# A gated layer's variance taken once per token, with tokens on partitions, and brought back by products with the identity

## The chip, the cores and the metric

The kernel runs on one core of one Trainium2 chip. The metric is the device time of one execution in microseconds (us): the median of three runs for the kernel before. A profiled execution, taken apart from these runs, gives the times of single instructions.

## The reference, cut to what matters

An image batch x of shape (4, 48, 256, 256) passes through four layers, each of the form x = x + layer(group_norm(x)). Layer 0 is a channel attention after a 3x3 depthwise convolution. Layer 1 is the gated layer that the change touches. Layers 2 and 3 are scans: down, up, right and left over the image with a five-tap convolution in each step. Of layer 1:

```python
t = x.reshape(B, H * W, dim)                   # 48 consecutive numbers of memory are one token
t = gelu(gelu(t @ W1 + b1))                    # 16 features per token
x1, x2 = t[..., :8], t[..., 8:]
n = (x2 - mean(x2)) / sqrt(var(x2) + 1e-5)     # over the 8 features of one token
sp = depthwise3x3(n) + dw_b; ch = pointwise(n) + pw_b
out = (x1 * (sp * ch)) @ W2 + b2
```

All arithmetic is in float32.

## The kernel before, in words

**Stages.** `layers01` first forms the attention's matrices of all four batches, and then, as a convolution with folded weights, layer 0's output y. The convolution is cut into 64 blocks of 16 image rows (4 batches of 16). Each block is done in two halves, each with full products (L581, tile py from x1n), smaller ones (L590, py from x2n), an add into y (L604) and its statistics (L605). The first 16 blocks run alone. The other 48 are interleaved with layer 1. `scans` does layers 2 and 3, in two chains (pairs of batches), each step six TensorE products (L1067, tile ps) and two adds on VectorE (L1071, L1075). The first chain begins under the last items of layer 1.

**The gated layer.** `gated_layer` works on 32 items of 32 image rows, 8 items a batch. With 16 strips of 8 features on the 128 partitions and 512 tokens of each strip along the free dimension, an item has tiles of 128x512. One call of `tick(c, ...)` does these steps for three items at once:

- for item c+1: `load` (the DMA to tok), `relay` (GpSimd's copy to pairs, L745), and `transposed` (six ptok tiles, 4 transposes each, L751, copied to xt by VectorE at L757 or ScalarE at L755);
- for item c: `hidden` (tile ph, L698, and Gelu on ScalarE, L768 to L779), `centered` (tile pm, L785: the mean over 8 features by a product with mean8; d on VectorE, L787; its square sq on GpSimd, L789), and `normed` (the part that changes, L791 to L807), which ends with ScalarE writing n (L801) and small DMAs of edge rows to near (L811 to L820);
- for item c-2: `shift` (GpSimd, L824), `gate` (psp and pch, L830 to L833, then sp and g), `output` (tiles pout, L868, and the adds into y, L879, in two parts), the DMA of y to x2, and `finish` (eight statistics, L900).

Four calls of `conv` in each tick put four convolution halves, that is two blocks, among these steps, as long as there are blocks left. After that a tick holds only its own steps and what a scan offers.

In `normed` before, L794 multiplies sq by mean8, a 128x128 matrix that averages each 8 neighbouring partitions and writes the average to all 8. So the variance of a token stands 8 times in pvar, and the root (L796, ScalarE), the reciprocal (L797, VectorE) and the product with d (L799, VectorE) are all on 128x512.

**Order and buffers.** The code calls the steps in the order of `tick`, and a scheduler decides each engine's final order when the kernel is built, by priorities and dependencies. Each engine then executes its own instructions in order. Wherever an instruction waits, everything behind it in that engine's queue waits too. The PSUM tiles named ph, pm, pvar, psp, pch, pout, ptok, and half of those named py, share a ring of 5 banks (pool `a_banks`, tag "bank"). sq and v have one buffer each. ScalarE loads a table of functions when it changes between Gelu and the root. In the profile such a load is named ACT_TABLE_LOAD. A float32 product is recorded as two TensorE passes.

Of the kernel before, what the change touches and what calls it, by code (L numbers as in the profile page):

```python
# [9 lines left out]
F32 = mybir.dt.float32  # L10
# [7 lines left out]
G = 16  # L18
# [9 lines left out]
F = 8  # L28
# [620 lines left out]
def gated_layer(ctx, tc, banks, p_small, x1, x2, w1, w2, dw, ends, pw, cols, b2, k, coef1, coef2):  # L649
# [6 lines left out]
    nc = tc.nc  # L656
    wp = ctx.enter_context(tc.tile_pool(name="t_w", bufs=1))
    tok = ctx.enter_context(tc.tile_pool(name="t_tok", bufs=1))
    feat = ctx.enter_context(tc.tile_pool(name="t_feat", bufs=2))
# [3 lines left out]
    CH = 2 * W  # L663
# [66 lines left out]
    h1s, h2s, ds, sqs, gs, xrs, ys, stats = {}, {}, {}, {}, {}, {}, {}, {}  # L730
# [59 lines left out]

    def normed(c):  # L791
        b, j = items[c]
        pv = banks.tile([128, CH], F32, tag="bank", name="pvar")
        nc.tensor.matmul(pv, lhsT=k["mean8", 128], rhs=sqs.pop(c), start=True, stop=True)  # L794
        v = feat.tile([128, CH], F32, tag="v", name="v", bufs=1)
        nc.scalar.activation(v, pv, AF.Sqrt, bias=eps)  # L796
        nc.vector.reciprocal(v, v)  # L797
        d = ds.pop(c)
        nc.vector.tensor_mul(d, d, v)  # L799
        n = n_sb[c % NN]  # L800
        nc.scalar.activation(  # L801
            n[:, :, 1 : W + 1].rearrange("p k (t q) -> p k q t", q=4),
            by_token(d),
            AF.Identity,
            bias=col[:, 3:4],
            scale=col[:, 2:3],
        )  # L807

        here, a, z = near[c % NN], slice(0, F), slice(F, 2 * F)
        top, last = n[0:F], n[128 - F : 128]  # L810
        nc.sync.dma_start(here[a, 1, :], last[:, 0, :])  # L811
        nc.sync.dma_start(here[z, 0, :], top[:, 1, :])
        if j == 0:
            nc.sync.dma_start(here[a, 0, :], zeros)
        else:
            nc.sync.dma_start(near[(c - 1) % NN][z, 1, :], top[:, 0, :])
        if j == NJ - 1:
            nc.sync.dma_start(here[z, 1, :], zeros)
        else:
            nc.sync.dma_start(near[(c + 1) % NN][a, 0, :], last[:, 1, :])  # L820
# [85 lines left out]
    def tick(c, conv, alone):  # L906
# [40 lines left out]
        if now:  # L947
            pieces.append(lambda: normed(c))
# [654 lines left out]
```

## Time and profile before

| | us |
|---|---|
| median of 3 runs (lowest to highest) | 8981.94 (8981.17 to 8982.99) |
| the profiled execution's own time | 8983.88 |
| its span, first to last instruction | 8982.1 |
| mean granted TensorE clock in it | 0.983 of full |
| busy in the span: PE, DVE, ACT, POOL | 8646.3, 4167.5, 3479.8, 1948.9 |
| `normed` for one item: L794's two passes, L796, L797, L799 | 1.02, 0.69, 3.34, 0.67 |

How to read it: PE is TensorE's matmuls, PEld its weight loads, DVE VectorE, ACT ScalarE, POOL GpSimd, SP the engine that issues most DMAs. L797 is line 797 of the kernel. A group is named by line, engine, operation, and output tile <- input tiles, followed by the shapes, the count, the busy time, the mean of one in ns, and the idle time of the engine just before these instructions with what ended it. A timeline line has the start in us, the length, and the same name, where x8 means eight instructions merged. In the list of waits, a line gives who waited for whom, the total in us, how often, and the longest. The slices are 40 equal parts of the span, with the busy share in tenths. Passes overlap in the records, so the spacing of two passes is less than the length of one. The gated layer's items run from about 2000 to about 3550 us. Convolution blocks are among them until about 3180 us.

### The profile page before, as it was taken

Reading aid. Unit: us, or ns where it says so; the run is one execution under the profiler, and the core shown is the slowest. Engines: PE = TensorE matmul, PEld = TensorE weight load, DVE = VectorE, ACT = ScalarE, POOL = GpSimd, SP = SyncE. Lnnn points to the kernel's source line nnn. Section 1 sums busy time; section 2 is a strip of 40 time slices with the busy share of each in tenths; the row PEclk is TensorE's granted clock in tenths of the full one; section 3 lists DMA queues with packets and bytes.
Section 4 is the critical chain, followed back from the end, with each engine's and each line's share of the span. In section 5 each row is a group of like instructions: output and inputs, shape, how many; then the busy total and the mean of one; then the engine's idle time right before and its main releaser. Section 6 shows DMA issues by size and latency. Waiting matters only on the chain. (4 is left out here: it accounts for less than half of the span.)

```text
span 8982.1 us, 162711 instructions
## 1 busy us (share of the span) xinstructions
PE 8646.3 (96%) x62920; PEld 7223.1 (80%) x62920; DVE 4167.5 (46%) x15625; ACT 3479.8 (39%) x7023; POOL 1948.9 (22%) x3100
## 2 busy tenths in 40 slices
PE   6999999999999978999999999999999999999998
PEld 4777777533333335999999999999999999999998
DVE  3231110234555555445666444445666555444653
ACT  0010101123433455766601776666663003665610
POOL 0000000001111111001454000001445664101575
PEclk9999999999999988999999999999999999999998
DMA  7654323367888876765577664556656887867789
GB/s 152 132 125 94 74 61 77 82 140 160 173 181 182 182 165 162 168 138 143 155 190 190 152 139 120 141 135 141 169 146 175 216 220 181 198 172 191 210 176 183
DMA packets 1180233, 1390.64 MB, mean 155 GB/s; under 512 B 263184, under 2 KB 1107216, under 8 KB 1118784
## 3 DMA queue, kind: packets, MB, share of 16 engines
q1 hardware_dynamic: 1179360, 1379.90, 65.7%
q8 instruction: 493, 8.08, 0.4%
q14 instruction: 284, 2.33, 0.1%
q0 software_dynamic: 96, 0.33, 0.0%
HBM read 811.21 MB, written 509.61 MB: 147 GB/s over the span
## 5 line engine op out<-in xcount | busy, mean ns | idle before, releaser
L1067 PE MATMUL ps<-carry,w 96*96 96x128 f32 x48960 | 5423.7, 273 | 59.3 <-DVE carry L1071 29.1
L1067 PEld LDWEIGHTS ps<-carry,w 96*96 96x96 f32 x48960 | 5397.6, 163 | 95.0 <-issue 44.9
L1264 POOL COPY pre<-col 96x256 f32<-96x256 f32 x1020 | 657.5, 646 | 2682.2 <-DMA col<-last 1964.1
L1153 ACT ACTIVATE dn<-carry,b 96x128 f32<-96x128 f32 (+1 forms) x2044 | 769.0, 398 | 796.8 <-DVE carry L1071 789.0
L1291 ACT ACTIVATE lines<-carry,b 96x128 f32<-96x128 f32 (+1 forms) x2044 | 819.8, 402 | 583.9 <-DVE carry L1075 574.0
L1071 DVE TENSOR_TENSOR carry<-ps,dn 96x128 f32<-96x128 f32 x2280 | 653.2, 288 | 806.1 <-PE ps L1067 781.2
L1199 ACT ACTIVATE up<-carry,b 96x128 f32<-96x128 f32 x1792 | 719.5, 402 | 459.9 <-DVE carry L1071 459.6
L1075 DVE TENSOR_TENSOR carry<-ps,lines 96x128 f32<-96x128 f32 x2040 | 576.8, 286 | 562.8 <-PE ps L1067 552.9
L1075 DVE TENSOR_TENSOR carry<-ps,pre 96x128 f32<-96x128 f32 x2040 | 586.7, 288 | 457.6 <-PE ps L1067 402.4
L1071 DVE TENSOR_TENSOR carry<-ps,up 96x128 f32<-96x128 f32 x1792 | 516.0, 288 | 598.1 <-PE ps L1067 592.8
L1339 POOL TENSOR_TENSOR stage<-stage,carry 96x256 f32<-96x256 f32 x768 | 657.4, 857 | 470.4 <-DVE seen L1044 436.7
L581 PE MATMUL py<-x1n,wy 128*96 128x512 f32 x1536 | 703.1, 607 | 30.9 <-ACT x1n L541 28.4
L295 PE MATMUL acc<-xs,xt 128*96 128x288 f32 x2048 | 667.2, 408 | 0.0
L294 PE MATMUL acc<-xt 128*96 128x288 f32 x2048 | 666.8, 409 | 0.0
L581 PEld LDWEIGHTS py<-x1n,wy 128*96 128x96 f32 x1536 | 244.2, 165 | 454.7 <-issue 437.1
L279 DVE COPY xt<-pt 128x384 f32<-128x384 f32 x256 | 136.7, 555 | 849.0 <-PE pt L276 645.8
L261 ACT ACTIVATE xn<-raw,coef 96x2048 f32<-96x2048 f32 x64 | 133.7, 2095 | 987.0 <-PE pt L276 819.6
L296 PE MATMUL acc<-xt,xs 128*96 128x192 f32 x2048 | 502.1, 327 | 0.0
L296 PEld LDWEIGHTS acc<-xt,xs 128*96 128x96 f32 x2048 | 332.4, 165 | 154.5 <-issue 1.8
L295 PEld LDWEIGHTS acc<-xs,xt 128*96 128x96 f32 x2048 | 332.2, 165 | 151.4 <-issue 2.8
L604 DVE TENSOR_TENSOR y<-py,t 96x512 f32<-96x512 f32 x256 | 171.4, 678 | 593.3 <-PE py L590 584.4
L590 PE MATMUL py<-x2n,wy 64*96 64x512 f32 x1536 | 363.0, 601 | 0.0
(186 smaller groups left out, 5542.7 us busy)
## 6 DMA issues: line engine op xcount, KB each, us to landing
stage<-x SPq DMA_DIRECT2D x64, 1536.0 KB
dn<-x SPq DMA_DIRECT2D x240, 384.0 KB
R<-lines SPq DMA_DIRECT2D x60, 1536.0 KB
lines<-R SPq DMA_DIRECT2D x60, 1536.0 KB
D<-dn SPq DMA_DIRECT2D x56, 1536.0 KB
up<-D SPq DMA_DIRECT2D x56, 1536.0 KB
U<-up SPq DMA_DIRECT2D x224, 384.0 KB
col<-U SPq DMA_DIRECT2D x56, 1536.0 KB
```

The costliest lines, as they stand in the source:

```text
L294: nc.tensor.matmul(acc[0], lhsT=xt[:, h + 2, :], rhs=xt[:, here, :], start=first, stop=last)
L295: nc.tensor.matmul(acc[1], lhsT=xt[:, h + 2, :], rhs=xs[:, here, :], start=first, stop=last)
L296: nc.tensor.matmul(acc[2], lhsT=xs[:, h + 2, :], rhs=xt[:, past, :], start=first, stop=last)
L581: nc.tensor.matmul(ps, lhsT=held["w"][0][:, dx], rhs=x1n[:, 2 * c : 2 * c + 2, dx : dx + W], start=dx == 0, stop=False)
L1067: nc.tensor.matmul(ps, lhsT=w_sb[layer][:, way, j, :], rhs=old[:, i, j : j + W // 2], start=j == 0, stop=j == 2)
L1071: nc.vector.tensor_add(new[:, i].rearrange("p (k w) -> p k w", w=KC), ps.rearrange("p (k w) -> p k w", w=KC), inp[:, i])
L1075: nc.vector.tensor_add(new[:, i], ps, inp[:, i])
L1153: nc.scalar.activation(inp[:, b], blocks(new[:, b]), AF.Identity, bias=bias[:, 0:1])
L1199: nc.scalar.activation(place[:, b], blocks(new[:, b]), AF.Identity, bias=bias[:, 1:2])
L1264: nc.gpsimd.tensor_copy(t, cols_view(block)[:, :, w % 2, :, w // 2])
L1291: nc.scalar.activation(line[:, b], new[:, b], AF.Identity, bias=bias[:, 2:3])
L1339: nc.gpsimd.tensor_add(to, to, new)
```

## The change

The variance is formed once per token, with tokens on partitions. sq is now the stationary operand, cut into four parts of 128 tokens, and the moving one is 16 columns of mean8 (each eighth column). The result, pvar, has 128 tokens on partitions and 4x16 values each, so root and reciprocal work on 128x64 instead of 128x512. GpSimd then copies each value 8 times into a new tile `wide` (128x512, one buffer), and four products with `wide` as the stationary operand and the identity as the moving one turn it back to features on partitions, in a new PSUM tile pstd of the same ring. The product with d reads pstd from PSUM where it read v from SBUF.

```diff
-        pv = banks.tile([128, CH], F32, tag="bank", name="pvar")
-        nc.tensor.matmul(pv, lhsT=k["mean8", 128], rhs=sqs.pop(c), start=True, stop=True)
-        v = feat.tile([128, CH], F32, tag="v", name="v", bufs=1)
+
+        pv = banks.tile([128, 4, G], F32, tag="bank", name="pvar")
+        sq = sqs.pop(c)
+        for q in range(4):
+            nc.tensor.matmul(
+                pv[:, q], lhsT=sq[:, 128 * q : 128 * q + 128], rhs=k["mean8", 128][:, 0:128:F], start=True, stop=True
+            )
+        v = feat.tile([128, 4, G], F32, tag="v", name="v", bufs=1)
         nc.scalar.activation(v, pv, AF.Sqrt, bias=eps)
         nc.vector.reciprocal(v, v)
+        wide = feat.tile([128, 4, G, F], F32, tag="wide", name="wide", bufs=1)
+        nc.gpsimd.tensor_copy(wide, v.unsqueeze(3).to_broadcast([128, 4, G, F]))
+        pb = banks.tile([128, 4, 128], F32, tag="bank", name="pstd")
+        for q in range(4):
+            spread = wide[:, q].rearrange("p g f -> p (g f)")
+            nc.tensor.matmul(pb[:, q], lhsT=spread, rhs=k["ident", 128], start=True, stop=True)
         d = ds.pop(c)
-        nc.vector.tensor_mul(d, d, v)
+        nc.vector.tensor_mul(d, d, pb.rearrange("p q n -> p (q n)"))
```

Lines of the changed kernel behind this place are 11 higher than before: the scans' products are L1078 there, pout L879.

## The prediction

> **What bounds the kernel now.** I read the page's busy times and slices first, then stretches of the span with the granted clock, then TensorE's waits, then the order of time through one tick of the gated layer.
>
> ```profile
> PE 8646.3 (96%) x62920; PEld 7223.1 (80%) x62920; DVE 4167.5 (46%) x15625; ACT 3479.8 (39%) x7023; POOL 1948.9 (22%) x3100
> PE   6999999999999978999999999999999999999998
> ```
>
> The group of the reciprocal in 1700 to 3000 us:
>
> ```profile
> L797 DVE RECIPROCAL v<-v 128x512 f32<-128x512 f32 x19 | 63.5, 3340 | 1.1 <-ACT v L796 1.1
> ```
>
> TensorE is busy 96% of the span and in nearly all slices: it is the bound, and a microsecond on its in-order queue is a microsecond of the span unless it replaces an idle one. The reciprocal that the change shrinks costs 3.34 us a tick, but on VectorE, which is half idle. So I ask what TensorE gains or loses.
>
> ```profile
> 2090.00:3180.00 1090.00, 1032.05 (x3795) 385.21 (x3794) 582.51 (x1006) 432.78 (x425) 163.38 (x327) 0.99 0.82 178
> 3180.00:3582.00 402.00, 318.31 (x1586) 174.37 (x1581) 230.12 (x505) 209.51 (x293) 67.03 (x73) 0.84 0.73 161
> ```
>
> Columns: stretch, length, busy of PE, PEld, DVE, ACT, POOL, granted clock, DMA share, GB/s. The first stretch holds 21 ticks (items 2 to 22, some 52 us each) in which the convolution's matmuls fill TensorE: only 58 us idle, 2.8 a tick. The second holds the last nine, with no convolution left: 84 us idle.
>
> ```profile
> PE py L581 <- ACT x1n L541: 27.9, 33, 1.1
> PE ptok L751 <- POOL pairs L745: 10.2, 12, 1.7
> ...
> PE ptok L751 <- DVE y L879: 4.6, 18, 1.0
> ...
> PE ptok L751 <- DVE y L879: 17.2, 6, 3.5
> ```
>
> These are TensorE's waits (total, times, longest), three of the first stretch and, last, one of the second. Only the waits on y have the reciprocal behind them (the y adds queue after it): 4.6 us, then 17.2 us in six waits.
>
> ```profile
> 2191.66 1.02 PE L794 MATMUL pvar<-sq,cst 128*128 128x512 f32 x2
> 2192.62 2.00 PE L868 MATMUL pout<-g,w_sb 32*96 32x512 f32 x8
> 2192.47 1.28 ACT L796 ACT_TABLE_LOAD   x1
> 2193.76 0.69 ACT L796 ACTIVATE v<-pvar,eps 128x512 f32<-128x512 f32 x1
> 2194.94 3.34 DVE L797 RECIPROCAL v<-v 128x512 f32<-128x512 f32 x1
> 2339.36 0.61 PE L718 MATMUL pstrip<-spread,cst 96*128 96x16 f32 x2 [2.31 <-DVE strip L720]
> 2339.81 1.95 PE L751 MATMUL ptok<-cst,pairs 128*128 128x128 f32 x8
> 2343.66 6.59 PE L581 MATMUL py<-x1n,wy 128*96 128x512 f32 x12
> ```
>
> In one tick, pvar is followed at once by pout: TensorE waits for nothing that root and reciprocal make. The last three lines are elsewhere: after 2.31 us without work, eight ptok passes take 1.95 us (1.09 otherwise) and twelve py passes 6.59 (5.36 otherwise). The stretch 2339.2 to 2346.0 has a granted clock of 0.51.
>
> **What the skill says.** "TensorE: Matmul & The Clock Gate", section "What's actually happening": activity is judged in windows of about 3.4 us, and the clock is halved after an idle one. The trace agrees in size (a wait of 2.31 us, then 6.8 us at half clock) but shows that less than a whole idle window is enough. The same page, "LDWEIGHTS (loading the stationary operand)": the load goes by weight columns, 128 / 1.2 = 107 ns, whatever the contraction depth. The trace: eighteen pw passes (L453, 48 moving columns, 128 weight columns) take 2.10 us, that is (2.10 - 0.27) / 17 = 0.108 us apart, with 0.27 for the last one's length. "ScalarE: Activation LUTs", "What ACT_TABLE_LOAD costs": 1283 ns and a drain of 1380 more. The trace has the 1.28 but no drain: the root starts 1.29 us after its load.
>
> **Part by part.** The order in which the changed kernel is compiled is known without a run, and decides this. In ticks 2 to 22 TensorE's queue reads ptok, pvar, pstd, pout, with nothing between pvar and pstd. pstd needs wide, wide needs v, v needs pvar: TensorE, in order, stands still for the round trip, and pout, the next py and ptok stand behind it.
>
> *Work on TensorE.* Removed: two passes of 512 columns, (5.36 - 0.61) / 11 = 0.43 us apart, 0.86. Added: pvar as four products, each two passes, with sq as weights of 128 columns: 8 x 0.11 = 0.9 although only 16 columns move; pstd 8 x 0.11 = 0.9. Net +0.93 us a tick.
>
> *The round trip.* The waits on both table load and root change place: in the compiled order the load itself waits for TensorE (before, it ran while pvar did). From pvar's end: 1.28 load; the root on 64 columns 0.31, on a line from 96x1 at 0.257 (L97) to 128x512 at 0.687; reciprocal 0.55, on a line from 96x1 at 0.156 (L98) to 128x512 at 3.339; POOL's copy: contiguous copies give 0.344 (128x192) and 0.396 us (96x256), 0.81 ns an element, so 0.60 for 512, while a strided one (L1264) takes 0.646 for 256, so 1.3: I take 0.65, near the low end, since the writes are contiguous. Four handovers of 0.03 to 0.08 make 0.2. Sum 3.0, and 0.16 that the last pass's length (0.27) exceeds its spacing (0.11): 3.15. VectorE is no later: its five operations ahead of the reciprocal end about 3.2 us after py's last pass, the root about 3.8. The compiled order has no load in three ticks (6, 14, 22), so the mean is 2.95. Bounds 2.6 to 3.6.
>
> *The clock.* In the second stretch, five waits of 2.84 to 3.5 us on y were followed by half-clock stretches of 3.4 or 6.8 us. The price read above: 0.86 + 1.23 = 2.1 us for one of 6.8 us. I take 1.9 per wait; bounds 1.0 and 2.8.
>
> *What gives way.* The idle that stood later in the tick: x1n's normalization now runs during the round trip or during ph (the compiled order moves pm behind a convolution half), so its 27.9 go; the 4.6 on y go, as the reciprocal no longer delays y; half of the 10.2 on pairs, as transfers get longer ticks. 37.6 / 21 = 1.8 us a tick; bounds 0.8 and all 2.8.
>
> *Sum, ticks 2 to 21.* 2.95 + 1.9 + 0.93 - 1.8 = 4.0 us, by 20 = 80. In tick 22 the wait lies ahead of a 21.2 us wait for y's transfers, which hides it: 0. Ticks 0 and 1 have 3.6 and 5.3 us of py between pvar and pstd, so work alone: 2.
>
> *Ticks 23 to 31.* Scan matmuls fill the gap (from 5.8 down to 1.8 us) in six of them; none or nearly none in 24, 29 and 30. Added: work 9 x 0.93 = 8.4; three waits near 3.0 with their clock, 14.6; the short cover of tick 26, 3.2; remnants 0.8. Removed: 17.2 on y and its clock, 5 x 1.9. Net 0, within 15 either way. POOL's copy joins a queue that is busy 15%: hidden, except on the round trip. PSUM's ring of five banks turns one bank further each tick: pout's last tile takes pvar's bank, free since the root, and the next ptok takes pstd's, free 0.7 us after pstd when d's product has read it, while pout alone runs 2.0 us: nothing. v's and wide's single buffers are reused a tick later: nothing; were pb's reader late by its own operations on VectorE, ptok would wait for it. SP's DMAs of the edge rows are the same ones, started at about the same point. The scans' compiled order on TensorE from row 4311 of 12412 is identical, so nothing further is due.
>
> Total +82 on the span of 8982.1: 9064. The profiled execution took 8983.9, and the median of the runs is 8981.9, 0.2 below the span, so **9063** as a median.
>
> **The rivals.** *Faster, by VectorE's relief:* in the second stretch all TensorE waits on y (24.7, 17.2 and 4.0 us) might come from a late VectorE; without the reciprocal they and their clock drops (9.5) go: -55, with +18 for work and remnants: -37. It decides if the first stretch costs less than 37 / 20 = 1.85 us a tick, that is if round trip and clock together stay below 1.85 + 1.8 - 0.93 = 2.7 us (a load hoisted ahead of pvar as before and an unbroken clock would do it). At a steady cost near 0: 8945. Against: 21.2 of the 24.7 is one wait for transfers, and the load waits on TensorE in the compiled order. *No change, transfers pace the stage:* the DMA share is 0.82, and a TensorE that waits for its transfers anyway could absorb the round trip. Then 8985. Against: transfers account for only 10.2 us of TensorE's waits in 1090. *Slower still:* a broadcast read on POOL as dear as the strided copy (3.6), 2.8 for the clock, only 0.8 given back: 6.5 x 20 + 2 + 15 = 147, so 9130. The change does do what it says: the compiled reciprocals are 128x64.
>
> **How the numbers follow.** Chances: forecast 0.74, faster 0.05, no change 0.06, slower still 0.15. About 0.2% (18 us) is what a measurement of this kernel can tell from no change. Low end: 2.6 + 1.0 + 0.93 - 2.8 = 1.7 a tick, by 20, plus 2, less 15 in the late ticks: +21, rounded out to 9000. High end into the slower case, 9125. Left out: both rivals on the low side and half of the slow one, 0.19.
>
> **What would show it.** Right: TensorE waits before pstd, named POOL wide, near 3 us in some 20 ticks; granted clock from 2090 us to item 22 near 0.95 instead of 0.99 (some 5 us at half in 57); waits on x1n nearly gone; pvar passes 0.11 apart; reciprocal near 0.55. Wrong: a wait below 2 us, a clock that stays at 0.99, or x1n's waits beside the new one.

## The result and the profile after

The changed kernel takes 9103.53 us (median of 4 runs, 9099.06 to 9109.92), the kernel before 8981.56 beside it on the same chip (4 runs, 8972.99 to 8982.99). The ratio is 1.0141, with a 95% interval of 1.0129 to 1.0154. The forecast was 9063, in a range of 9000 to 9125: the side and the range hold, but the growth was 122 us where 82 was forecast. The profiled execution took 9101.23 us, its span is 9099.4, 117 us more than before; the sums by stage below are of these profiled spans.

The page of the changed kernel, busy times and slices, first. TensorE is as full as before over the whole span, but six slices fall below nine tenths where two did; VectorE lost 84 us and the span grew all the same.

```profile
PE 8690.1 (96%) x63368; PEld 7290.3 (80%) x63368; DVE 4083.0 (45%) x15625; ACT 3459.6 (38%) x7023; POOL 1962.0 (22%) x3132
PE   6999999999888878999999999999999999999998
```

The two stretches that the forecast read, now in the changed kernel (columns as there):

```profile
2090.00:3180.00 1090.00, 969.06 (x3648) 391.22 (x3647) 474.97 (x896) 371.45 (x377) 152.00 (x307) 0.92 0.75 159
3180.00:3582.00 402.00, 330.49 (x1635) 171.97 (x1634) 196.11 (x442) 190.43 (x248) 83.26 (x102) 0.87 0.75 163
```

In 1090 us TensorE is busy 969 instead of 1032, at a granted clock of 0.92 instead of 0.99, and it gets through fewer passes. Since the changed kernel is later in its work at the same time, I count from here on by items: from the start of item 2's pvar to that of item 22's (twenty ticks, the first stretch), then to 30 us after item 31's pvar (the late ticks), then the rest.

| span of | before | after | difference |
|---|---|---|---|
| start to item 2's pvar | 2139.2 | 2133.5 | -5.7 |
| first stretch, twenty ticks | 1044.8 | 1174.9 | +130.1 |
| late ticks | 342.1 | 332.9 | -9.2 |
| rest (scans) | 5456.1 | 5458.2 | +2.1 |
| all | 8982.1 | 9099.4 | +117.3 |

So all of the growth is in the first stretch, 6.5 us a tick. The waits of TensorE there, in the changed kernel (who waited for whom, total us, times, longest):

```profile
PE ptok L751 <- POOL pairs L745: 70.9, 19, 4.2
PE pstd L808 <- POOL wide L804: 59.4, 20, 3.1
PE pstrip L718 <- DVE strip L720: 4.3, 2, 2.2
```

The second line is the forecast wait: 2.97 us, twenty times. The waits on x1n (27.9 us before), on y (4.6) and on xt ahead of pout (8.6 in 13 waits) are gone. The first line is a surprise. It was 10.2 us before, and I had let half of it vanish; it is now the largest.

One tick of the changed kernel in order of time, with the engines of the round trip and, ahead of it, what leads to the wait on pairs:

```profile
2290.92 1.12 PE L785 MATMUL pm<-h,cst 128*128 128x512 f32 x2
2292.94 0.67 DVE L787 TENSOR_TENSOR d<-h,pm 128x512 f32<-128x512 f32 x1
2293.70 1.04 POOL L789 TENSOR_TENSOR sq<-d 128x512 f32<-128x512 f32 x1 [8.09 <-DVE d L787]
2294.68 2.87 POOL L745 COPY pairs<-tok 128x1536 f32<-128x1536 f32 x2
2296.20 1.97 PE L751 MATMUL ptok<-cst,pairs 128*128 128x128 f32 x8 [4.15 <-POOL pairs L745]
...
2308.89 0.96 PE L797 MATMUL pvar<-cst,sq 128*128 128x16 f32 x8
2309.93 1.28 ACT L801 ACT_TABLE_LOAD   x1 [7.36 <-PE pvar L797]
2311.22 0.31 ACT L801 ACTIVATE v<-pvar,eps 128x64 f32<-128x64 f32 x1
2311.57 0.55 DVE L802 RECIPROCAL v<-v 128x64 f32<-128x64 f32 x1 [0.32 <-ACT v L801]
2312.26 0.61 POOL L804 COPY wide<-v 128x512 f32<-128x512 f32 x1 [1.79 <-DVE v L802]
2312.92 1.77 PE L808 MATMUL pstd<-cst,wide 128*128 128x128 f32 x8 [3.07 <-POOL wide L804]
2314.62 2.04 PE L879 MATMUL pout<-g,w_sb 32*96 32x512 f32 x8
```

The lower half is the forecast chain, link by link: load 1.28, root 0.31, reciprocal 0.55, copy 0.61, and 3.07 us in which TensorE does nothing. pstd then takes 1.77 us for what takes 1.15 in pm_early_warm, a run below in which TensorE doesn't stop ahead of it. The upper half was not forecast. pm ends at 2292.04; VectorE has work of the convolution (L605, L604) to do first, so d is begun at 2292.94; GpSimd's queue holds sq and then pairs. GpSimd has been idle for 8.09 us when d ends and sq starts, with pairs behind it, and TensorE waits 4.15 us for the first half of pairs. In the kernel before, pairs did not start behind sq but when its own transfer had landed:

```profile
2435.72 1.04 POOL L789 TENSOR_TENSOR sq<-d 128x512 f32<-128x512 f32 x1
2441.89 2.87 POOL L745 COPY pairs<-tok 128x1536 f32<-128x1536 f32 x2 [5.13 <-DMA tok<-x]
```

### The profile page after: what moved, and what is told of

Same layout as the page of the kernel before. It is cut to its first block, busy times and chain, and to the rows that moved or that the text cites. A ratio compares the mean times of both kernels' runs of the same rounds, so it can differ in the third digit from the quotient of the medians.

```text
span 9099.4 us, 163597 instructions
## 1 busy us (share of the span) xinstructions
PE 8690.1 (96%) x63368; PEld 7290.3 (80%) x63368; DVE 4083.0 (45%) x15625; ACT 3459.6 (38%) x7023; POOL 1962.0 (22%) x3132
## 5 line engine op out<-in xcount | busy, mean ns | idle before, releaser
L1078 PE MATMUL ps<-carry,w 96*96 96x128 f32 x48960 | 5425.4, 273 | 65.2 <-DVE carry L1082 30.5
L1078 PEld LDWEIGHTS ps<-carry,w 96*96 96x96 f32 x48960 | 5397.3, 163 | 95.2 <-DVE carry L1086 38.5
L604 DVE TENSOR_TENSOR y<-py,t 96x512 f32<-96x512 f32 x256 | 172.8, 677 | 630.4 <-PE py L590 624.5
```

The lines of the kernel that those rows point to most:

```text
L1078: nc.tensor.matmul(ps, lhsT=w_sb[layer][:, way, j, :], rhs=old[:, i, j : j + W // 2], start=j == 0, stop=j == 2)
```

## The experiments

The main theory after the first look: TensorE's order with pm behind a convolution half delays d and sq, and GpSimd's queue, where pairs stands behind sq, passes the delay on to ptok (the queue theory). The rival: pairs is late because of its transfers. The round trip and its half clock (stretches in which TensorE is granted half of its full clock) are then priced by themselves. Sums in the first stretch are always counted from item 2's pvar to item 22's of the kernel named. Each ratio is to the kernel before as measured beside that run: 8978.3 us for pm_early, pm_early_warm, no_wait and split_late, 8975.9 for the other four. So differences between runs that were not measured together are good to some us only.

**pm_early: pm ahead of the convolution half, as before the change.**

```diff
-        pieces.append(conv)
         if now:
             pieces.append(lambda: centered(c))
+        pieces.append(conv)
```

> The changed kernel with one step moved: the mean's product pm is called ahead of the tick's first convolution half instead of behind it, so that in the compiled order it follows pch at once, as it did before the change; everything else is in the same order. Theory (GpSimd's queue): in the changed kernel pm stands behind a convolution half of some 8 us, d and GpSimd's square wait for it, and the copy to pairs stands behind the square in GpSimd's queue, so TensorE's 70.9 us of waits on pairs in the first stretch (10.2 before) come from the order and not from transfers. Then the waits on pairs fall to 10 to 20 us, some 25 us of half clock behind them go too, up to 28 us of waits on x1n come back: 9015 to 9040 us. Rival (transfers): the tok tiles land late anyway, the copy then waits for its DMA, and the time stays at 9095 to 9110.

Measured: 9032.55 us, ratio to the kernel before 1.0064 (1.0048 to 1.0081). Its waits in the first stretch:

```profile
PE pstd L808 <- POOL wide L804: 59.4, 20, 3.1
PE ptok L751 <- POOL pairs L745: 24.3, 15, 2.0
```

The wait on wide is the same to the tenth, that on pairs falls from 70.9 to 24.3, and 71 of the 122 us go. The 24.3 are a little above the 10 to 20 expected, and no wait on x1n came back. The arithmetic of the change is untouched, so about 71 us belong to where pm stands. The rival of the transfers falls for these.

**pairs_first: TensorE's order left as in the changed kernel, GpSimd's turned round.** pm_early moves more than one queue. Here the orders of TensorE and ScalarE stay the same down to the last instruction, and VectorE's but for a small copy and an add that change places; only GpSimd does pairs ahead of sq, by a copy of 8 columns that sq must come after.

```diff
+        if c + 1 < len(items):
+            nc.gpsimd.tensor_copy(sq[:, 0:8], pairs[c + 1][:, 0, 7, 0:8])
         nc.gpsimd.tensor_mul(sq, d, d)
```

> The changed kernel with TensorE's compiled order kept as it is (pm behind the convolution half), and only GpSimd's order turned round: a copy of 8 columns from pairs into sq's tile, ahead of the square, forces the pairs copy in front of sq. Queue theory (TensorE's 70.9 us of waits on pairs come from the pairs copy standing behind sq in GpSimd's queue): with tok mostly landed by then, these waits fall below 25 us, half-clock stretches fall with them, and the time to 9030 to 9065. Rival (pairs is late for its transfers, or because pm's move delays everything else): the waits stay above 55 us and the time above 9085.

Measured: 9025.23 us, 1.0053 (1.0040 to 1.0065), 5 us below the range expected; the span of the first stretch is 1097.5 us instead of 1174.9. First its waits, then GpSimd's part of one tick:

```profile
PE pstd L808 <- POOL wide L804: 59.4, 20, 3.1
PE ptok L751 <- POOL pairs L745: 22.1, 16, 2.0
```

```profile
2567.54 2.88 POOL L745 COPY pairs<-tok 128x1536 f32<-128x1536 f32 x2 [5.17 <-DMA tok<-x]
2570.36 0.19 POOL L790 COPY sq<-pairs 128x8 f32<-128x8 f32 x1
2570.63 1.04 POOL L791 TENSOR_TENSOR sq<-d 128x512 f32<-128x512 f32 x1
```

pairs now starts when tok has landed. One engine's order, changed by an instruction of 0.19 us, gives back 78 of the 122 us (9103.5 - 9025.2; 73 when each is counted from the kernel before beside it). The queue theory is shown. With it the half clock shrinks too: the trace's records of the granted clock give 189.6 us at half in the first stretch of the changed kernel, 95.0 here, 25.5 before.

**pm_early_warm: the round trip stays, but TensorE is kept at work in it.** Four products of 440 columns, whose result is overwritten, stand ahead of pstd in pm_early.

```diff
+WARM = 4
...
+        for _ in range(WARM):
+            nc.tensor.matmul(
+                pb.rearrange("p q n -> p (q n)")[:, :440], lhsT=k["mean8", 128], rhs=k.t[:, 0:440], start=True, stop=True
+            )
         for q in range(4):
             spread = wide[:, q].rearrange("p g f -> p (g f)")
```

> The same, and between pvar and pstd TensorE does four products of 440 columns whose result is overwritten by pstd (3.0 us of TensorE work at full clock, where it would otherwise wait 3.0 us). Output unchanged. Theory (the wait costs its own length and then a lower clock): the wait is only filled, so what is saved against the kernel without the filling is the clock alone, 1.6 us in some 20 ticks: 25 to 40 us less than it, and few half-clock stretches between 2090 and 3250 us. Rival (the half clock comes from other waits, or filling delays pstd): the same time as without the filling within 8 us, or more.

Measured: 8989.48 us (20 runs), 1.0013 (1.0006 to 1.0019): 43 us less than pm_early, for work that is thrown away, and a little more than the 25 to 40 expected. The first stretch by length, busy times and clock, pm_early first, this kernel second:

```profile
2134.91:3245.24 1110.33, 1016.49 (x3907) 408.72 (x3905) 517.19 (x982) 402.53 (x407) 168.18 (x330) 0.95 0.79 168
```

```profile
2128.71:3199.11 1070.40, 1036.19 (x4066) 419.50 (x4065) 518.10 (x983) 403.16 (x407) 168.15 (x330) 0.99 0.82 175
```

The same twenty ticks take 1070.4 us instead of 1110.3, with a clock of 0.99 instead of 0.95. The other waits are no shorter (24.8 us on pairs), and the filler takes 3.15 us a tick, a little more than the wait of 2.97 that it fills. So (1110.3 - 1070.4) / 20 = 2.0 us is about the price of the clock after one wait of 3 us. The two profiled executions are 65 us apart (9041.7 and 8976.4), the medians 43. By the medians the price would be 43 / 24 = 1.8 us, with the four waits of the late ticks counted in. About 2, then, and not sharper.

**no_wait: pstd multiplies a constant, so nothing waits for the round trip.** It leaves out the product with the root's reciprocal (d is multiplied by another number); all other work stays. As compiled, its pm stands directly after pch, as in pm_early.

```diff
-            spread = wide[:, q].rearrange("p g f -> p (g f)")
-            nc.tensor.matmul(pb[:, q], lhsT=spread, rhs=k["ident", 128], start=True, stop=True)
+            nc.tensor.matmul(pb[:, q], lhsT=k["ones", 128], rhs=k["ident", 128], start=True, stop=True)
```

> The changed kernel with pstd's four products taken from a constant matrix of ones instead of wide: root, reciprocal and GpSimd's copy still run but nothing waits for them; the normalization by the standard deviation is left out of the result. TensorE's work is that of the changed kernel. Theory (work 0.93 us an item, the rest waits): +30 us for 32 items, less up to 15 us that VectorE's relief brings in the last ticks: 8990 to 9015. Rival (the products themselves are dear, their weights of 128 columns loaded at 0.2 us each): 9035 or more.

Measured: 9019.39 us, 1.0052 (1.0037 to 1.0067), a little above what was expected. Its largest waits in the first stretch:

```profile
PE py L581 <- ACT x1n L541: 43.6, 33, 1.9
PE ptok L751 <- POOL pairs L745: 18.8, 16, 4.6
PE pout L878 <- DVE xt L757: 6.5, 12, 0.9
```

The 59.4 us on wide are gone, and 43.6 us on x1n stand there: with nothing to hide behind, ScalarE's normalization of the next block is late again, more than before the change (27.9). Beside pm_early, which has pm in the same place, only 13 us are gained (9032.6 to 9019.4) though 59.4 us of waits go: here most of a wait that was taken out of a full queue is replaced by the next ones. Half clock still takes 47.8 us of the first stretch, against 109.2 in pm_early. In this kernel the compiled order of ptok and py differs, too, so the 13 us are not the price of the wait alone.

**split_late: pstd after the next convolution half and ptok,** so that the round trip has cover.

```diff
+        wides[c] = wide
+
+    def scaled(c):
+        b, j = items[c]
+        wide = wides.pop(c)
         pb = banks.tile([128, 4, 128], F32, tag="bank", name="pstd")
...
         if new:
             pieces += [lambda i=i: transposed(c + 1, i) for i in range(4, NI)]
+        if now:
+            pieces.append(lambda: scaled(c))
```

> The changed kernel with its step cut in two: pvar, root, reciprocal and copy stay where they were, pstd, the product with d and what follows are called behind the next convolution half and the last ptok tiles. In the compiled order pout and two ptok tiles, some 3.0 us, lie between pvar and pstd. Output unchanged. Theory (the round trip costs only because nothing lies under it): TensorE's waits on wide fall below 10 us in all and the time is within 12 us of that of the kernel that does not wait for wide: 8990 to 9020. Rival (a bank of the ring held longer, or n later, gives the time back): 9040 to 9080.

Measured: 9026.09 us, 1.0060 (1.0045 to 1.0075): above the range expected, within 7 us of no_wait. No wait on wide is left in the first stretch (2.5 us in the late ticks), but one on pairs:

```profile
PE ptok L751 <- POOL pairs L745: 49.3, 20, 3.3
```

GpSimd in one tick of it:

```profile
2442.81 3.87 POOL L840 COPY nears<-near 16x512 f32<-16x512 f32 x6
2449.92 1.26 POOL L855 TENSOR_TENSOR g<-h,sp 128x512 f32<-128x512 f32 x1 [3.24 <-DVE sp L853]
2451.13 2.87 POOL L745 COPY pairs<-tok 128x1536 f32<-128x1536 f32 x2
```

Its compiled pm is directly after pch, so this isn't pm's delay. With pstd later, n and its edge rows (near) are later, and as compiled the copies to nears stand behind sq in GpSimd's queue; the last product of psp, which needs nears, is compiled behind eight convolution products; sp and g follow it, and pairs stands behind g. By this order it is the same mechanism through another instruction: what is moved on one engine comes back through GpSimd's queue. No run tried this link alone.

**var_early: pm early, and cover for the round trip.** pm is directly after pch as compiled; pvar comes after the first pout, and a whole convolution half and a ptok lie between pvar and pstd.

```diff
+    def scaled(c):
...
-        pieces.append(conv)
         if now:
             pieces.append(lambda: centered(c))
+        pieces.append(conv)
...
+        if now:
+            pieces.append(lambda: normed(c))
         pieces.append(conv)
...
         if now:
-            pieces.append(lambda: normed(c))
+            pieces.append(lambda: scaled(c))
```

> The changed arithmetic in another order: pm directly after pch as before, pvar after the first pout with a whole convolution half and a ptok between it and pstd. Theory (round trip, clock and the pairs queue are the cost, and the work alone is small): no wait on wide, granted clock 0.98 or more in the first stretch, work of 20 x 0.93 = 19 us added, and the smaller reciprocal takes back part of it (waits on y 4.6 and 17.2 us before): 8965 to 9000. Rival (the added products or one more bank of PSUM in use always cost another wait, as in split_late): 9015 or more.

Measured: 9006.61 us, 1.0032 (1.0019 to 1.0045), the best order found without filler, 7 us above the range and below the rival's 9015. In its first stretch:

```profile
PE ptok L751 <- POOL pairs L745: 25.6, 15, 2.3
PE py L581 <- DVE y L895: 16.8, 14, 2.2
```

As expected, no wait on wide in this stretch (8.1 us in four waits are left in the late ticks). The wait of py on VectorE's y adds is new, 16.8 us: py's next tile follows pvar directly and, by the name of the wait, takes a bank of the ring that those adds still read. So the rival had a part of the truth. The clock is 0.97, where 0.98 or more was expected.

**pm_early_noroot: pm_early with a shorter round trip.**

```diff
-        nc.scalar.activation(v, pv, AF.Sqrt, bias=eps)
+        nc.scalar.activation(v, pv, AF.Identity, bias=eps)
```

> pm_early, with the root left out: the activation that writes v keeps its shape but is an Identity, so no table is loaded for it; its output is therefore not the reference's. Chain theory: the wait before pstd is the sum of its links, so it falls by the load's 1.28 us to about 1.7 us in 20 ticks, 26 us in all, and shorter waits call the half clock less often (up to 2.0 us each): 8970 to 9010, against 9032 for pm_early. Rival (the wait is ended by VectorE's or GpSimd's own queue, with the load hidden behind it): the wait stays above 2.5 us and the time within 10 us of pm_early's.

Measured: 9037.87 us, 1.0066 (1.0051 to 1.0082), the same as pm_early within the noise. The expectation fails. One round trip of it:

```profile
2358.94 0.68 DVE L757 COPY xt<-ptok 128x512 f32<-128x512 f32 x1
2359.54 0.68 DVE L605 BATCH_NORM_STATS2 st<-y 96x6 f32<-96x512 f32 x1
2360.14 0.53 DVE L802 RECIPROCAL v<-v 128x64 f32<-128x64 f32 x1
```

```profile
2358.85 0.31 ACT L801 ACTIVATE v<-pvar,eps 128x64 f32<-128x64 f32 x1 [8.09 <-PE pvar L797]
```

v is there at 2359.16, but the reciprocal starts at 2360.14, when VectorE has worked off its queue. So the load's 1.28 us are not worth 1.28: the wait before pstd is 51.1 / 20 = 2.56 us instead of 2.97, since the reciprocal now waits for a second condition, a free VectorE, and that comes only 0.4 us before v was ready with the load. This is what the rival said. That second condition was in the forecast, with 0.6 us of slack (3.2 against 3.8 us); I did not use it for this expectation. The first stretch is 13.8 us shorter than pm_early's, and the late ticks are 15.0 longer, with 39.0 us of waits on pairs there instead of 16.8, in a compiled order of their own. That the late ticks always give back what the first stretch gains isn't shown: pairs_first is short in both.

**before_norecip: VectorE's relief alone,** the kernel before with less work on VectorE and none added elsewhere.

```diff
-        nc.vector.reciprocal(v, v)
```

> The kernel before with the reciprocal left out (so d is multiplied by the root itself; the output isn't the reference's): VectorE's relief alone, without anything added to TensorE. My forecast gave it 4.6 us of waits on y in the first stretch and, in the last nine ticks, 17.2 us of waits on y with 9.5 of half clock: 8950 to 8978. If VectorE's reciprocal holds up nothing, 8975 to 8990; if it lay on the path of every tick (20 x 3.34), below 8930.

Measured: 8986.06 us (21 runs), 1.0012 (1.0005 to 1.0018): 3.34 us less of VectorE's work a tick make the kernel 10 us slower, not up to 26 faster; it lies in the range given for a reciprocal that holds up nothing. The first fence is the kernel before in the late ticks, the second this one.

```profile
PE pout L868 <- DVE y L879: 24.7, 3, 21.2
PE ptok L751 <- DVE y L879: 17.2, 6, 3.5
PE ptok L751 <- POOL pairs L745: 9.7, 1, 9.7
```

```profile
PE ptok L751 <- POOL pairs L745: 37.3, 4, 10.5
PE pout L867 <- DVE y L878: 25.9, 1, 25.9
PE ptok L751 <- DVE y L878: 2.3, 6, 0.9
```

The 17.2 us on y shrink to 2.3, as forecast, and 27.6 us more on pairs take their place. In the first stretch x1n's waits grow from 27.9 to 35.3, and those on y stay (5.3 us, 4.6 before): the reciprocal was not what held y up there. VectorE was late for work that something else would have held up too. The compiled order of this kernel differs in places, so the 10 us are those of relief and new order together; a gain hidden in it was not seen.

## Why the prediction was right in side and range, and 40 us short

**The round trip**: right. 3.0 us forecast (mean 2.95), 2.97 measured, with its links at 1.28, 0.31, 0.55 and 0.61 against 1.28, 0.31, 0.55 and 0.65. The copy of GpSimd with a broadcast read was the unknown (0.60 to 1.3); it cost what a contiguous one does.

**The clock**: the price per wait was right, 1.9 forecast and about 2.0 measured by pm_early_warm. The number of waits was not: those on pairs call the half clock too. In the first stretch the changed kernel has 39 stretches at half clock, pm_early 27 and the kernel before 6. The longest wait just ahead of them is in 20 of the 39 the one on wide, in 17 one on pairs. TensorE's busy time there, without the filler's 63 us, is 973.2 in pm_early_warm, 1016.5 in pm_early and 1038.1 in the changed kernel: 43 us of clock behind the round trip (38 forecast), and 22 more behind pairs (29 if counted from pairs_first's 1009.3).

**Work on TensorE**: right. From the start of pvar to the start of pout, no_wait, with no wait between, takes 1.88 us a tick and the kernel before 0.96 for its pvar: 0.92 more, forecast 0.93.

**What gives way**: this is the step that failed. The forecast read: "half of the 10.2 on pairs, as transfers get longer ticks". The compiled order was in front of me: pm behind a convolution half. I counted that move only where it helps, for x1n, and never followed pm's own chain: d, sq, and what stands behind sq on GpSimd. The waits on pairs rose by 60.7 us instead of falling by 5. Against that, more gave way than I had said. x1n's 27.9 went as forecast, and the round trip is the likely cause: they stay away in pm_early, where pm is back in its old place, and return in no_wait, where nothing waits for wide. y's 4.6 went too, but not for the reason given: without the reciprocal alone (before_norecip) they stay. Waits of pout on xt went as well (8.6), and pout's own busy time falls from 83.1 to 63.5 us in pm_early_warm at a clock like that of before. The forecast had "nothing" for PSUM's ring, and the ring does not explain this: in no_wait, where pstd takes its bank too, pout still waits 6.5 us on xt and is busy 85.8. That VectorE gets on with its copies while TensorE stands or does filler would fit both runs, but the order of ptok and py differs in no_wait, and no run tried it alone.

**The sum for the first stretch**: idle time +59.4 (wide) +60.7 (pairs) -42.4 (the others) = +77.7; busy time +64.9 for the clock and -12.5 for the rest (the added work, less what pout and py lost) = +52.4. Together 130.1, where 80 was forecast. On the error of 50: pairs +66, clock +27, and about -43 for what else gave way. So the range held with some luck: two misses of +93 and -43 lay on either side.

**Ticks 0 and 1, 22 to 31**: forecast +2 and 0 within 15, measured -5.7 ahead of item 2 and -9.2 from item 22 on. The waits on y went there as forecast, and of the 21.2 us in tick 22, which the forecast had left in place, 4.6 are left; a wait of 16.3 on pairs stands where 9.7 stood. Ticks 0 and 1 and the late ones give back 17 of the 50, and the scans add 2: 35 of error in the profiled span (117 less 82), 40 by the medians.

**The rivals**: faster by VectorE's relief falls (before_norecip: no gain even without the change's costs). No change by transfers falls too: TensorE did not absorb the round trip, whose 59.4 us stand in full beside the 70.9 on pairs, and with its order kept and pairs ahead of sq, the transfers leave 22.1 of these. Slower still named a dear copy on GpSimd, a dearer clock and less given back; the copy was cheap and the clock's price as forecast, so the time came near its 9130 for another reason.

## What to carry to other kernels

When a scheduler moves one instruction, follow it in every queue: what waits for its result, and what stands behind that waiter on an in-order engine. Here a product of 0.9 us, moved behind 8 us of other products, cost 78 us in all, with its half clock; the wait that the change was known to add cost 59.4 us, and some 100 with its own. What a relieved engine is worth is what the next condition leaves, here nothing: take the relief alone as an experiment before counting on it.

## What the runs showed of the hardware that was not expected

- Half clock follows waits shorter than its own length: 20 waits of 2.56 us on the mean, with others of at most 2.1, still gave 25 stretches of mostly 3.4 us (pm_early_noroot, first stretch), and 20 of 2.97 gave 27 (pm_early); a half-clock stretch began in each of these 40 waits or within 3.4 us of its end, but so at most with 4 of pm_early's 16 shorter waits ahead of ptok (2.0 us or less). Five of the 27 lasted 6.8 us. In each trace every change of the granted clock from 2000 to 3600 us lies on a grid of 3.413 us, to within 3 ns, and in the step of the grid ahead of each of pm_early_noroot's 25 stretches TensorE's records have it busy for 0.8 to 2.7 us. That agrees in size with the windows in "TensorE: Matmul & The Clock Gate", section "What's actually happening" (the Trainium skill), but not with the need for a whole idle one. What share of a step must be idle is not settled here: steps with 2.1 us busy kept the full clock in the same run.
- Thrown-away products can pay: 63 us of filler in the twenty ticks, on the bound engine, went with a kernel 43 us faster than pm_early, though still 11 us slower than the kernel before.
- GpSimd's copy with each value read 8 times takes 0.610 us for 128x512, VectorE's reciprocal 0.549 for 128x64 against 3.340 for 128x512. Eight passes with 128 weight columns and only 16 moving ones take 0.96 us: (0.96 - 0.26) / 7 = 0.10 us apart, where 0.11 was forecast.
